# Three streams of one convolution pipeline, re-timed: taps paced by emitted work, attention begun a band earlier, rows loaded band by band

## The chip, the cores and the metric

The kernel runs on one core of a Trainium2 chip. The metric is the device time of one execution in microseconds (us). Three runs of the kernel before took 10178.35, 10182.17 and 10183.77 us, median 10182.17.

## The reference

Two layers over x of shape (32, 96, 56, 56), fp32. Layer 0 is an inverted bottleneck with squeeze-and-excite; layer 1 is a chain of Fourier attention, a deformable 3x3 convolution beside a plain one, and a batch norm over all 32 images.

```python
# layer 0
h = silu(bn(conv1x1(x, fake_quant(w1))))                 # 96 -> 576 channels
h = silu(bn(depthwise3x3(h, fake_quant(w2))))
s = sigmoid(se_w2 @ silu(se_w1 @ mean(h) + b1) + b2)
x = x + bn(conv1x1(h * s, fake_quant(w3)))               # 576 -> 96
# layer 1
mag = abs(rfft2(x)); ca = sigmoid(mlp(pooled convs of mag))     # per channel
sa = sigmoid(convs of (mean x, l2 x, resized mean of mag))      # per pixel
y = x * ca * sa
freq = resize(mean(abs(rfft2(y))))
aux = concat(y, coord, freq)
offset = conv3x3(aux); gate = sigmoid(conv(relu(conv3x3(aux))))
y_def = 9 taps of y sampled bilinearly at offset, times def_w
z = (1 - gate) * conv3x3(y) + gate * y_def
out = relu(batch_norm(z) + x)                            # statistics over all images
```

## The kernel before, in words

Every image goes through three stages, and three images are in work at once. The innermost is the **band loop** (`for n, (b, j) in enumerate(bands)`, L1134): image `b` is cut in 7 bands `j` of 8 rows. A band is done in two halves `h`, each in two groups of tiles. Beside it run two Python generators, `streams`: `second(b + 1)` is `attend` for the next image (squeeze, the 1x1 projection, two Fourier passes `dft_mag`, the small convolutions of the attention), and `first(b + 2)` is `hidden` for the image after that (expand on TensorE, depthwise taps on VectorE).

Engines run their queues in the order in which this Python code emits instructions (`manual_schedule`), so *when* a generator is advanced decides the order of work on every queue. The clock of that order is the **slot**: `pump()` (L1029) counts one slot up and advances the streams. A band has 17 slots (14 in the two halves, 3 at its end), an image 119. A `yield` in a generator is one slot. Slots are not equal in time: the band's own work on TensorE (the joint convolution L632 at the band's start, sampling L738, `deform` L757, transposes L724, base convolution L670) is put out in slots 0, 3, 7 and 10; slots 11 to 16 hold hardly any.

- `hidden` (L221): 9 units of 128 channels by 28 rows; a unit is 9 taps on VectorE (L284, L286), one a step, with the next unit's expand (L186, evacuated by ScalarE with silu at L190 into one of two buffers `hp`) put in between. `finish` (L238) applies silu and stores the unit as `h2d`. Before, the 81 taps of an image are spread evenly over its 119 slots (`due`, L1033).
- `attend` (L444): starts with `squeeze` (L304); then 4 projections of 14 rows (loads L333, matmuls L351 and L357, evacuation L362, residual on GpSimd L474, store to `x1d` L475); a Fourier pass (loads L380, matmuls L407 and L432); then a chain of small matmuls into one PSUM tile `acc` (L488 to L569). Each of them waits for ScalarE or VectorE to read what the one before it wrote: a **hop**. Then a second Fourier pass on the gated image and a last short chain (L593, L599) whose result `fqd` is the frequency row. Before, most hops are one slot apart.
- `refill` (L1056): loads rows of the next image's `x1d` into the one padded image `yp` (L611, on SyncE's queue), the spatial attention as `sab` (L613, on GpSimd's queue, two buffers), and later multiplies on VectorE (`attend_rows`, L619); then loads the frequency row (L623). Rows of image `b+1` overwrite rows of image `b` that are no longer read.
- `offsets` (L646): joint convolution of band `n + 2`, evacuation, the copy `at` on VectorE (L661), its store `od` on GpSimd's queue (L665), base convolution, the broadcast load `ht` on SyncE's queue (L681), two activations (L683, L684) and the store `hd` (L686). `weights_load` (L690) reads `hd` on SyncE's queue; `weights` (L704) multiplies on VectorE.

The **turn** is band 5 (`turn = NBD - 2`, L1023): from there `offsets` of band `n + 2` belongs to the next image, so its rows must be in `yp`. Before, at the turn `drain()` runs out what is left of both streams, `refill` and `flush` follow, and both streams are started anew for the next pair of images. The attention thus begins at band 5 (first work three slots on) and ends in band 3 of the next image, some 90 slots later; rows 0 to 37 are all loaded in slot 10 of band 4.

Of the kernel before, what the change touches and what calls it, by code (L numbers as in the profile page):

```python
# [20 lines left out]
RB = 8  # L21
# [9 lines left out]
PD = 2  # L31
# [45 lines left out]
WAIT = object()  # L77

# [142 lines left out]
def hidden(tc, p, x, xn, h2d, pooled, defer):  # L221


    nc = tc.nc
    w = p["w0"]

    def rows_of(x, half):
        xt = p["xt"].tile([C, (HH + 1) * W], FP, name="xt")
        r0 = half * (HH - 1)
        nc.sync.dma_start(xt, x[:, r0 : r0 + HH + 1].rearrange("c h w -> c (h w)"))  # L230
        return xt

    xts = p.pop("xts", None) or [rows_of(x, 0), rows_of(x, 1)]
    if not p.pop("expanded", False):
        for _ in expand(nc, p, xts, UNITS[0]):
            yield

    def finish(u, acc):  # L238
        ch = UNITS[u][0]
        flat = acc.rearrange("p h w -> p (h w)")  # L240
        nc.scalar.activation(flat, flat, AF.Silu, bias=w["sh2"][:, ch : ch + 1], scale=w["inv2"][:, ch : ch + 1],  # L241
                             accum_out=pooled[:, u : u + 1])
        nc.scalar.dma_start(h2d[u], flat)

    before = None
    for u, (ch, half) in enumerate(UNITS):
        h1 = p["h1"]
        if xn is not None and u in (5, 8):

            p.setdefault("xts", []).append(rows_of(xn, int(u == 8)))  # L250
        if u + 1 < len(UNITS):
            more = expand(nc, p, xts, UNITS[u + 1])
        elif xn is not None:
            more = expand(nc, p, p["xts"], UNITS[0])
            p["expanded"] = True
        else:
            more = iter(())
        acc = p["acch"].tile([128, HH, W], FP, name="acch")

        rows_of_tap = lambda dy: (int(half == 0 and dy == 0), HH - int(half == 1 and dy == 2))  # L260
        diag = p.get("diag")
        taps = [k for k in (4, 0, 1, 2, 3, 5, 6, 7, 8) if diag is None or k not in TPE]
        parts = []
        if diag is not None:
            for r0 in range(0, HH, ER):
                pt = bank(p)[:, :EW].rearrange("p (h w) -> p h w", h=ER)
                for i, k in enumerate(TPE):
                    dy, dx = divmod(k, 3)
                    lo, hi = rows_of_tap(dy)
                    lo, hi = max(r0, lo), min(r0 + ER, hi)  # L270
                    nc.tensor.matmul(pt[:, lo - r0 : hi - r0], diag[:, ch, i], h1[:, dy + lo : dy + hi, dx : dx + W],
                                     start=(i == 0), stop=(i == len(TPE) - 1))
                parts.append((slice(r0, r0 + ER), pt))
            yield
        for n, k in enumerate(taps):
            dy, dx = divmod(k, 3)
            lo, hi = rows_of_tap(dy)
            win = h1[:, dy + lo : dy + hi, dx : dx + W]
            wk = w["w2"][:, ch, k : k + 1]
            if n == 0:  # L280
                for rs, pt in parts:
                    nc.vector.scalar_tensor_tensor(acc[:, rs], win[:, rs], wk, pt, ALU.mult, ALU.add)
                if not parts:
                    nc.vector.tensor_scalar(acc, win, wk, None, ALU.mult)  # L284
            else:
                nc.vector.scalar_tensor_tensor(acc[:, lo:hi], win, wk, acc[:, lo:hi], ALU.mult, ALU.add)  # L286
            if n == 3 and before:
                finish(u - 1, before)
            if len(taps) - 8 < n < len(taps) - 1:
                next(more, None)  # L290
            yield
        for _ in more:
            pass
        before = acc
    defer(lambda: finish(len(UNITS) - 1, before))
# [8 lines left out]
def squeeze(nc, p, pooled):  # L304
# [6 lines left out]
    yield  # L311
    s1 = p["sp"].tile([RED, 1], FP, name="s1")
    nc.scalar.activation(s1, p1[:RED, 0:1], AF.Silu, bias=w["seb1"], scale=1.0 / HW)
    yield
    for ch in range(NCH):
        nc.tensor.matmul(p1[:, 8 + ch : 9 + ch], w["sew2"][:, ch], s1, start=True, stop=True)
    yield
# [3 lines left out]
    yield  # L321
# [45 lines left out]
def dft_mag(nc, p, src, gate=None):  # L367
# [28 lines left out]
    if gate is None:  # L396
        parts = p["sq"].tile([2 * WX, 2, NPB * V], FP, name="sq")[: 2 * H, :, : NG * W].rearrange("p k (g w) -> p k g w", g=NG)
        yield from wait(2)
# [21 lines left out]
    yield  # L420
# [3 lines left out]
    for q0 in range(0, NP // 2, NQB):  # L424
# [14 lines left out]
        yield  # L439
    p["magnitude"] = mag  # L440
    yield from at_conv(p, lambda: nc.scalar.activation(mag, mag, AF.Sqrt))


def attend(tc, p, b, x, h2d, pooled, x1, given=False):  # L444
# [5 lines left out]
    nc = tc.nc  # L450
    w = p["w"]
    if not given:
# [6 lines left out]
        for q in range(NQ):  # L459
# [4 lines left out]
            yield  # L464
            if q + 1 < NQ:
                first = project_loads(nc, p, h2d, q + 1, 0)
            next(outs)
            yield
            os = next(outs)
            if q + 1 < NQ:  # L470
                rows = [first, project_loads(nc, p, h2d, q + 1, 1)]
# [5 lines left out]
        yield from wait(2)  # L477
# [3 lines left out]
    yield from dft_mag(nc, p, x1)  # L481
    mag = p["magnitude"]

    pa = p["acc"].tile([128, 512], FP, name="acc")
# [3 lines left out]
    nc.tensor.matmul(pm, w["fold"], p["sums"].rearrange("p k w -> p (k w)"), start=True, stop=True)  # L488
# [3 lines left out]
    s3 = p["sp"].tile([H, 2, W], FP, name="s3")  # L492
    nc.scalar.activation(s3[:, 1], pm[:, W:], AF.Sqrt, bias=w["eps6"][:H], scale=1.0 / C)
    nc.scalar.mul(s3[:, 0], pm[:, :W], 1.0 / C)
# [11 lines left out]
    yield  # L506
# [6 lines left out]
    yield  # L513
# [8 lines left out]
    yield  # L522
# [4 lines left out]
    yield  # L527
# [4 lines left out]
    yield  # L532
# [6 lines left out]
    yield  # L539
# [6 lines left out]
    yield  # L546
# [9 lines left out]
    yield  # L556
# [13 lines left out]
    yield  # L570
# [3 lines left out]
    yield  # L574
# [19 lines left out]
    yield  # L594
    fy = p["sp"].tile([V, 2, W], FP, name="fy")
    nc.scalar.copy(fy.rearrange("p m w -> p (m w)"), pf)
    yield
    for m in range(2):
        nc.tensor.matmul(pz, w["rows2"][:, m], fy[:, m], start=(m == 0), stop=(m == 1))  # L599
    yield  # L600
# [45 lines left out]
def offsets(nc, p, yp, j, top, hid, ybs, hds):  # L646
# [11 lines left out]
    yield  # L658
# [19 lines left out]
    yield from wait(2)  # L678
# [277 lines left out]
def layers(tc, a, dp, x1d, zd, stats, far):  # L956
# [6 lines left out]
    nc = tc.nc  # L963
    B = x1d.shape[0]
    with ExitStack() as ctx:
        p = {"tc": tc, "dp": ctx.enter_context(tc.tile_pool(name="l1d", bufs=3, space=DRAM))}
# [25 lines left out]
        streams, later = [], []  # L992
# [31 lines left out]
        n_first = len(UNITS) * NTAP  # L1024

        def start(b, length):
            streams[:] = [[second(b + 1), 0, slot + 3], [first(b + 2), 0, slot, length]]

        def pump():  # L1029
            nonlocal slot  # L1030
            slot += 1
            for st in streams:
                due = slot - st[2] if len(st) == 3 else n_first * (slot - st[2]) / st[3]  # L1033
                while st[1] < due:
                    if next(st[0], None) is WAIT:
                        break
                    st[1] += 1
                    if len(st) == 3:
                        break
            later.sort(key=lambda e: e[0])  # L1040
            while later and later[0][0] <= slot:
                later.pop(0)[1]()

# [5 lines left out]
        def drain():  # L1049
            for st in streams:  # L1050
                for _ in st[0]:
# [81 lines left out]
        start(0, turn * (NTX + 3))  # L1133
        for n, (b, j) in enumerate(bands):  # L1134
            if j == 0:
                st = p["st"].tile([C, NBD, 6], FP, name="st")
            if j == turn:
                drain()
                refill(b + 1, j * RB - PD)
                flush()  # L1140
                start(b + 1, slots)
            more = find(n + 2) if n + 2 < len(bands) else iter(())
            next(more, None)
            release()
            for h in range(2):
# [3 lines left out]
                for i, group in enumerate(GROUPS):  # L1149
# [4 lines left out]
                    if i == 0:  # L1154
# [10 lines left out]
                        if b + 1 < B and j == turn - 1 and h == 1:  # L1165
                            refill(b + 1, turn * RB - PD)
# [365 lines left out]
```

## Time and profile before

| what | value |
|---|---|
| median of three runs | 10182.17 us |
| the profiled execution | 10207.2 us, span 10205.2 us |
| mean granted TensorE clock | 0.888 |
| first joint convolution at | 377.4 us |
| last instruction before the closing normalisation (chain starts) | about 9925 us |
| the closing normalisation (L1357 to L1365) | about 280 us, bound by its loads and stores |

So some 9,550 us are the band loop, 32 images of about 300 us. The costliest groups of VectorE, TensorE and GpSimd in it:

```profile
L286 DVE SCALAR_TENSOR_TENSOR acch<-hp,w,acch 128x1512 f32<-128x1512 f32 (+1 forms) x2250 | 4222.5, 1877 | 37.8
L632 PE MATMUL mm<-yp,c_jointW 104*128 104x448 f32 x4032 | 1729.9, 585 | 420.7 <-DMA yp<-fqd 296.2
L714 POOL COPY ybl<-yp 96x448 f32<-96x448 f32 x896 | 980.6, 1120 | 3598.6 <-PE mm L724 3598.6
```

A row gives line, engine, operation, tiles, shapes and count; then the busy time in us and the mean of one in ns; then the idle time of the engine just before these instructions, and who ended it. The first row is the depthwise taps: 2250 of 1.88 us, more than half of VectorE's work. An fp32 matmul of the program shows as two records, so 4032 records are 2016 matmuls.

### The profile page before, as it was taken

The numbers are of one execution on the slowest core, as the hardware profiler recorded it, in microseconds if no ns is written. First come the engines' busy times: TensorE is split into PE (matmuls) and PEld (weight loads), VectorE is DVE, ScalarE is ACT, GpSimd is POOL, SyncE is SP. The second block draws the span as 40 slices with busy tenths as digits, with TensorE's granted clock in tenths as the row PEclk, the third lists the DMA queues.
The fourth block names the chain that finished last, engine by engine and source line by source line (L and its number), as shares of the span: only waits on it lengthen the run. The fifth ranks groups of instructions, "written<-read, shape, count | busy, mean of one in ns | idle before, by whom it ended". The sixth has DMA issues, their size and how long they took to land. (4 is left out here: it accounts for less than half of the span.)

```text
span 10205.2 us, 129758 instructions
## 1 busy us (share of the span) xinstructions
PE 8493.2 (83%) x48374; PEld 5169.5 (51%) x48374; DVE 7226.4 (71%) x6948; ACT 5318.3 (52%) x10264; POOL 2490.8 (24%) x2642
## 2 busy tenths in 40 slices
PE   5888888888888888888888888888888888888870
PEld 3455555555555555555555555555555555555540
DVE  7677777777767777777777777777777777777323
ACT  2355555555555555555555555555555555555443
POOL 0122222222222222222222222223222222322110
PEclk9888989998888988898898898898889889988985
DMA  2455455555455555555555555555555555545449
GB/s 77 115 139 138 135 144 153 146 146 128 136 141 144 152 148 137 134 139 143 151 145 145 130 137 141 143 151 151 134 135 138 144 150 150 150 129 135 126 129 418
DMA packets 1069475, 1486.00 MB, mean 146 GB/s; under 512 B 590438, under 2 KB 840086, under 8 KB 1056550
## 3 DMA queue, kind: packets, MB, share of 16 engines
q1 hardware_dynamic: 858747, 985.20, 37.4%
q10 hardware_dynamic: 153803, 329.80, 8.9%
q0 software_dynamic: 56288, 162.60, 6.5%
q8 instruction: 388, 6.36, 0.3%
q14 instruction: 249, 2.04, 0.1%
HBM read 1064.29 MB, written 412.65 MB: 145 GB/s over the span
## 5 line engine op out<-in xcount | busy, mean ns | idle before, releaser
L286 DVE SCALAR_TENSOR_TENSOR acch<-hp,w,acch 128x1512 f32<-128x1512 f32 (+1 forms) x2250 | 4222.5, 1877 | 37.8
L632 PE MATMUL mm<-yp,c_jointW 104*128 104x448 f32 x4032 | 1729.9, 585 | 420.7 <-DMA yp<-fqd 296.2
L714 POOL COPY ybl<-yp 96x448 f32<-96x448 f32 x896 | 980.6, 1120 | 3598.6 <-PE mm L724 3598.6
L757 PE MATMUL pd<-v,c_def 128*96 128x224 f32 (+1 forms) x6272 | 1431.1, 385 | 64.4 <-DVE z L796 61.4
L632 PEld LDWEIGHTS mm<-yp,c_jointW 104*128 104x128 f32 x4032 | 812.3, 204 | 1261.0 <-issue 1158.4
L742 ACT COPY v<-mm 96x288 f32<-96x288 f32 (+1 forms) x2688 | 996.3, 442 | 805.7 <-PE mm L738 756.5
L757 PEld LDWEIGHTS pd<-v,c_def 128*96 128x96 f32 (+1 forms) x6272 | 1098.7, 179 | 427.3 <-issue 130.6
L190 ACT ACTIVATE hp<-mm,sh,inv 128x392 f32<-128x392 f32 (+2 forms) x1216 | 801.2, 673 | 892.1 <-PE mm L186 702.3
L186 PE MATMUL mm<-xt,w 96*128 96x392 f32 (+3 forms) x2688 | 1058.2, 546 | 51.6 <-DMA xt<-in_x 45.6
L738 PE MATMUL mm<-wc,yt 64*96 64x144 f32 x12544 | 1053.4, 302 | 31.5 <-ACT hp L190 16.3
L738 PEld LDWEIGHTS mm<-wc,yt 64*96 64x96 f32 x12544 | 837.8, 166 | 351.2 <-issue 175.8
L670 PE MATMUL mm<-yp,c_base0W 96*64 96x448 f32 x4032 | 974.5, 585 | 0.0
L726 ACT COPY yt<-mm 128x384 f32<-128x384 f32 (+1 forms) x896 | 348.8, 441 | 1060.7 <-PE mm L724 1060.1
L351 PE MATMUL mm<-hq,w3s 128*96 128x392 f32 x2048 | 740.5, 508 | 137.1 <-DMA hq<-h2d 105.9
L661 DVE COPY at<-mm 18x224 f32<-18x224 f32 x448 | 154.4, 380 | 972.8 <-ACT yb L657 970.2
L749 ACT COPY v<-v 32x448 f32<-32x448 f32 x1344 | 755.3, 562 | 40.7 <-ACT ht L684 16.2
L665 POOL DMA_DIRECT2D od<-at x224 | 185.1, 826 | 2286.3 <-DVE at L661 2095.4
L407 PE MATMUL mm<-c_FU,x 112*128 112x116 f32 x3072 | 443.6, 299 | 264.9 <-DMA x<-x1d 224.9
L241 ACT ACTIVATE acch<-acch,sh,inv 128x1568 f32<-128x1568 f32 x288 | 487.5, 1693 | 300.4 <-DVE acch L286 287.2
L704 DVE TENSOR_TENSOR wc<-wc,wr 128x1008 f32<-128x1008 f32 x448 | 591.8, 1321 | 25.0 <-PE mm L724 9.4
L670 PEld LDWEIGHTS mm<-yp,c_base0W 96*64 96x64 f32 x4032 | 339.1, 143 | 529.2 <-issue 454.8
L474 POOL TENSOR_TENSOR o<-o,xc 96x392 f32<-96x392 f32 x256 | 438.7, 1714 | 672.4 <-ACT o L362 622.0
(195 smaller groups left out, 9108.7 us busy)
## 6 DMA issues: line engine op xcount, KB each, us to landing
h2d<-acch ACTq DMA_DIRECT2D x288, 784.0 KB
wc<-hd SPq DMA_DIRECT2D x896, 252.0 KB
wr<-hd SPq DMA_DIRECT2D x896, 252.0 KB
hq<-h2d SPq DMA_DIRECT2D x128, 980.0 KB
hq<-h2d SPq DMA_DIRECT2D x128, 784.0 KB
x<-x1d SPq DMA_DIRECT2D x768, 98.0 KB
ht<-od SPq DMA_DIRECT2D x224, 252.0 KB
hd<-ht ACTq DMA_DIRECT2D x224, 252.0 KB
```

Source lines behind the costliest of these rows:

```text
L186: nc.tensor.matmul(pt[p0 : p0 + w1.shape[1], : rows * W], w1, xts[hf][:, r0 * W : (r0 + rows) * W], start=True, stop=True)
L190: nc.scalar.activation(h1[lo:hi, row0 : row0 + rows, 1 : 1 + W], pt[lo:hi, : rows * W].rearrange("p (h w) -> p h w", h=rows), AF.Silu, bia ...
L286: nc.vector.scalar_tensor_tensor(acc[:, lo:hi], win, wk, acc[:, lo:hi], ALU.mult, ALU.add)
L351: nc.tensor.matmul(pts[half][:C, :EW], w3s[:, ch], hq, start=(i == 0), stop=False)
L632: nc.tensor.matmul(view, weights[:, k], yp[:channels, r0 : r0 + RB, dx + PD - 1 : dx + PD - 1 + W], start=(k == 0), stop=(k == NTAP - 1))
L670: nc.tensor.matmul(pb[k % 2 * BC : (k % 2 + 1) * BC, :BW].rearrange("p (h w) -> p h w", h=RB), w["base"][:, k], yp[:C, r0 : r0 + RB, dx + ...
L704: nc.vector.tensor_tensor(wc, wc, wr, ALU.mult)
L714: nc.gpsimd.tensor_copy(yb[:, :, s], blocks)
L738: nc.tensor.matmul(pt[k][:C, (t - lo) * KP : (t - lo + 1) * KP], yt[ps, t], s[ps, t * KP : (t + 1) * KP], start=True, stop=True)
L742: nc.scalar.copy(v[:C, :, lo:hi, k].rearrange("c k t p -> c t k p"), pt[k][:C, : (hi - lo) * KP].rearrange("c (t k p) -> c t k p", t=hi - ...
L749: nc.scalar.copy(v[C:, 1 + 2 * i : 3 + 2 * i], v[i * QC : (i + 1) * QC, KA:])
L757: nc.tensor.matmul(out.rearrange("c q (t x) -> c t q x", x=TS), p["w"]["def"][ks, k], v[ks, k].rearrange("c t s (r x) -> c t (s r) x", r=T ...
```

## The change

1. **Pacing.** A `Clock` counts, at emission, an estimate of the TensorE and VectorE time of every instruction of the band loop (wrappers `Counted` and `Engines` around `nc.tensor` and `nc.vector`). The depthwise stream is no longer advanced by slots: at the end of each `pump` it is advanced until the emitted VectorE time since the start stands to the emitted TensorE time as 232.0 to 220.4.
2. **Start.** Both streams are drained and restarted at band 4 (`PHASE`), after that band's joint convolution is emitted, in place of band 5 before it.
3. **Hops.** 18 plain `yield`s in `squeeze`, `attend` and `dft_mag` become `yield from wait(2)`. The wait ahead of the first Fourier pass's matmuls is one slot shorter, the wait after the last projection one longer; projection loads are issued one slot earlier; in `offsets`, the `at` copy and with it the `od` store come one slot later, `ht` stays. The `fold` matmul and the l2 root move into the Fourier pass.
4. **Rows.** `refill` runs in bands 2, 3 and 4 (up to rows 22, 30, 38), in the first half, in place of once in band 4's second half (up to row 38).

The number of instructions of each kind is the same. Core of the diff:

```diff
+class Clock:
+    def count(self, engine, args):
+        free = lambda t: math.prod(t.shape[1:])
+        aps = [t for t in args if hasattr(t, "shape")]
+        if engine == "pe":
+            out, w = aps[0], aps[1]
+            share = 0.5 ** ((w.shape[0] <= 64) + (math.prod(w.shape[1:]) <= 64))
...
+            self.pe += max(max(free(out), 48) * 1.7e-3 * share, 0.158 if w.shape[0] == 64 and share == 0.5 else 0.0)
+        else:
+            self.dve += (max(map(free, aps)) + 180) / 960
...
@@ attend
             next(outs)
-            yield
             if q + 1 < NQ:
                 first = project_loads(nc, p, h2d, q + 1, 0)
+            yield
             next(outs)
+            if q + 1 < NQ:
+                rows = [first, project_loads(nc, p, h2d, q + 1, 1)]
             yield
...
-        yield from wait(2)
+        yield from wait(3)
...
@@ squeeze, dft_mag, attend: 18 times
-    yield
+    yield from wait(2)
...
@@ offsets
-    yield
+    yield from wait(2)
     at = p["off"].tile([NOFF, NTX, 2, TP], FP, name="at")
...
-    yield from wait(2)
+    yield
     ht = p["ht"].tile([SB * NTX, 4, KP], FP, name="ht")
...
@@ layers
-        def start(b, length):
-            streams[:] = [[second(b + 1), 0, slot + 3], [first(b + 2), 0, slot, length]]
+        PHASE, PE_IMAGE, DVE_IMAGE = NBD - 3, 220.4, 232.0
+        def start(b, share=1.0):
+            streams[:] = [second(b + 1), first(b + 2)]
+            paced[:] = clock.pe, clock.dve, share * PE_IMAGE
         def pump():
             slot += 1
-            for st in streams:
-                due = slot - st[2] if len(st) == 3 else n_first * (slot - st[2]) / st[3]
-                while st[1] < due:
...
+            next(streams[0], None)
             later.sort(key=lambda e: e[0])
             while later and later[0][0] <= slot:
                 later.pop(0)[1]()
+            while clock.dve - paced[1] < (clock.pe - paced[0]) / paced[2] * DVE_IMAGE:
+                if next(streams[1], paced) is paced:
+                    break
...
-        start(0, turn * (NTX + 3))
+        start(0, 0.83)
...
+            more = find(n + 2) if n + 2 < len(bands) else iter(())
             if j == turn:
-                drain()
                 refill(b + 1, j * RB - PD)
                 flush()
-                start(b + 1, slots)
-            more = find(n + 2) if n + 2 < len(bands) else iter(())
             next(more, None)
             release()
+            if j == PHASE:
+                drain()
+                start(b + 1)
...
-                        if b + 1 < B and j == turn - 1 and h == 1:
-                            refill(b + 1, turn * RB - PD)
+                        if b + 1 < B and 1 < j < turn and h == 0:
+                            refill(b + 1, (j + 1) * RB - PD)
```

## The prediction

> **What bounds the kernel now.** I read the page's first two parts, then the busy time by windows, then the waits of TensorE.
>
> ```profile
> PE 8493.2 (83%) x48374; PEld 5169.5 (51%) x48374; DVE 7226.4 (71%) x6948; ACT 5318.3 (52%) x10264; POOL 2490.8 (24%) x2642
> ...
> PEclk9888989998888988898898898898889889988985
> ```
>
> TensorE leads, no engine is full, and the granted clock stays near 0.9 throughout. The windows (columns: window, us, then busy us of PE, PEld, DVE, ACT, POOL, then granted clock, DMA share, GB/s):
>
> ```profile
> 1003.30:9426.90 8423.60, 7295.53 (x41936) 4443.64 (x41937) 6253.59 (x5769) 4558.52 (x8872) 2220.69 (x2296) 0.90 0.53 142
> 5205.00:5226.00 21.00, 8.74 (x39) 5.11 (x38) 16.50 (x13) 8.85 (x17) 4.84 (x6) 0.67 0.87 201
> 5083.00:5115.00 32.00, 23.93 (x147) 16.58 (x146) 20.95 (x27) 17.70 (x42) 3.07 (x5) 0.68 0.42 110
> 5267.00:5290.00 23.00, 23.00 (x106) 12.00 (x105) 5.92 (x6) 9.74 (x18) 10.79 (x14) 1.00 0.60 198
> ```
>
> The first is 28 images: 300.8 us each, TensorE busy 260.6, VectorE 223.3, so 40.2 us of TensorE idle. The second is one turn, the third one attention chain, the fourth a stretch without gaps. Where TensorE idles the clock is granted at 0.67, where it does not at 1.00. The clock records hold only the values 1.0 and 0.5: laid over the busy intervals, 61.8 us of each image run at half clock, 44.5 of them while TensorE is busy. That loses up to 44.5 / 2 = 22 us, so an image is about 238.5 us of matmul at full clock, 22 us of slow clock and 40 us of idle. Each us of idle drags 22/40 = 0.55 us of slow clock behind it. I check the 238.5: start-to-start times at full clock by row (joint convolution 2 x 0.389 us a matmul, deform 2 x 0.193, projection 2 x 0.342, ...) times the counts give 238.6. VectorE's 223 us are 15 us under it.
>
> The waits of TensorE between 400 and 9900 us, 31 images (total us, times, longest):
>
> ```profile
> PE mm L632 <- DMA yp<-fqd: 291.9, 26, 12.6
> PE mm L407 <- DMA x<-x1d: 222.4, 55, 6.9
> PE mm L351 <- DMA hq<-h2d: 102.1, 73, 4.9
> PE acc L538 <- ACT s L535: 67.7, 31, 2.5
> PE mm L632 <- ACT hp L190: 64.6, 29, 2.2
> PE pd L757 <- DVE z L796: 61.4, 38, 2.0
> PE mm L632 <- DVE acch L286: 59.9, 5, 12.7
> PE acc L316 <- ACT s L313: 55.4, 31, 3.2
> PE acc L518 <- ACT fe L508: 46.9, 31, 1.5
> PE acc L526 <- ACT t L524: 41.2, 30, 1.4
> PE acc L599 <- ACT fy L596: 36.7, 31, 1.4
> PE acc L563 <- ACT ca L562: 33.6, 31, 2.4
> ```
>
> Three things: the turn (rows 1 and 7), loads for the Fourier pass and the projection (2, 3), and the hops (`acc`). So the bound is TensorE's in-order queue, standing still at points where the emitted order brings a consumer too close behind its producer.
>
> **The change part by part.** Nothing is computed anew; what moves is the distance, in TensorE work, between producer and consumer. I took the new order from the built program and weighed each instruction with its row's mean of the trace before.
>
> *Turn and rows.* Before, rows 0 to 37 are asked for in slot 10 of band 4, and the joint convolution that reads them stands 7 slots on, with some 4 us of TensorE work between. After, the last rows it reads are loaded in band 2, 48 slots ahead, and the frequency row 14 slots ahead. Rows 1 and 7 go: (291.9 + 59.9) / 31 = 11.3 us an image. Each row chunk's issues (L611 median 0.53 us on SyncE, L613 about 0.51 us on GpSimd) are the same in number, only spread.
>
> *Drain.* Before, what is left of the taps is emitted in one lump at the turn. After, the streams end almost together: one or two taps are drained.
>
> *Pacing.* Emitted work by band, us of TensorE / VectorE, band 0 to 6. Before: 40/42, 31/38, 37/29, 27/33, 25/30, 36/30, 43/30. After: 27/24, 34/33, 30/31, 26/26, 33/29, 51/50, 37/39. The sum of the larger of each band is 259 before, 241 after. But before the waits on VectorE are small, so little of the 18 us is there to win: the waits for `hp`, `z` and ScalarE's evacuations, (64.6 + 61.4 + some 34) / 31 = 5.2 us an image. Bounds: 0 and 5.2; I take 2.5, half, as the balance cannot touch those that are pure distance.
>
> *Hops.* The `acc` waits add up to 350 us, 11.3 an image. Before, `sew2` has 2.1 us of matmuls between it and its producer and waits 1.8: the hop is about 3.9 us. After, 3.5 to 4.3 lie between: gone. L518 (4.6 us cover, 1.5 wait; after 8.6), L526 (half), L599 (no cover, 1.2; after 2.8 to 3.6), L563 (5.2, 1.1; after 10.5) go too: together 6.3 us. But a second slot is worth only what TensorE work is emitted in it: L538, L544 and L550 now fall in slots 13 to 17 of band 0, which hold none, and ScalarE's own work (L683, L684 at 0.78 us each, three packs of 0.56) stands in their hops. They keep their 3.9 us, and L569 now stands behind six taps (6 x 1.88 = 11.3 us on VectorE beside about 10 us on TensorE): I charge 3 us. Net 3.3; bounds 0 and 10.
>
> *Fourier loads.* All of the 7.2 us an image is at two places: the first group (2.7) and the sixth (5.4, where only two groups of 0.92 us stand between the buffer's release and its reuse). After, about 19 us of TensorE work stand between the last projection and the first group, against 15 + 2.7 = 17 needed: gone. The sixth stays: its buffer is released by VectorE's sums (L391), now behind five taps. Gain 2.2.
>
> *Projection loads.* A slot earlier and in the densest band (51 us): 102.1 + 25 over 31 is 4.1; I take 3.1.
>
> *Costs.* `od` is now behind the two block copies (2 x 1.1 us) on GpSimd's queue, and in band 2 behind a third `sab` load that waits for a buffer until `attend_rows`, three slots on. Then `ht`, L683 and `hd` come late. The trace shows `ht` landing 2 to 9 us after its issue and L683 never waiting (0.5 us in all), so I cost it at 0 to 5 us once an image and take 0, since ScalarE comes to L683 only at about 27 of band 2's 30 us. Image 0: its streams are drained in band 4 with some 42 of the attention's 112 slots left, serial, about 45 us once.
>
> *A rule against the row.* "TensorE: Matmul & The Clock Gate" of the Trainium skill (Why this matters for your kernels) says that only idle gaps over some 3 us throw the clock back to half. By it, of what I remove only the turn's waits count, and their half clock lies inside the idle itself: no clock comes back. The trace says otherwise: in the attention chain above no gap exceeds 1.9 us, yet the clock is 0.68, and 133 of 183 gaps of 1.5 to 2.5 us have half clock within 3.5 us. The measurement decides.
>
> *Sum.* Idle removed: 11.3 + 2.5 + 3.3 + 2.2 + 3.1 = 22.4 us an image. With 0.55 of slow clock: 34.7. Times 31: 1076 us. Against the profiled execution: 10207 - 1076 + 45 = 9176. The median of the runs stands 25 us under it: **9150 us**. By the rule the sum is 10182 - 31 x 22.4 + 45 = 9533.
>
> **Rivals.** *A, the waits nearly vanish.* Balanced bands and longer distances leave only matmul at full clock and about 11 us: 250 us an image, 10182 - 31 x 51 + 45 = 8650. For it: VectorE has 15 us to spare, and emitted VectorE never gains over 10 us on TensorE within a few slots. Against: the uncovered hops and the sixth Fourier group.
>
> *B, only the turn goes.* The hops and loads give back what they win, and the clock returns for the turn alone or as the rule says: 11 to 14 us an image: 10182 - 31 x 13 + 45 = 9820. For it: shorter slots give each DMA less time. Against: the distances in TensorE work, which grew.
>
> *C, slower.* The `at` copy (L661) frees the joint convolution's PSUM bank. It stands a slot later, behind 4 to 7 taps emitted together (7.5 to 13 us); six banks rotate, and the first half's sampling and transposes take eight, so TensorE stops there when VectorE is behind. Cover is about 11 us: the price is some 2 us a band as emitted. To lose the 34.7 it takes 5 us a band, 7 times. For it: VectorE waits 970 us for `yb` before L661 today, so that copy is on a chain. Against: taps need no fresh matmul and run ahead during the joint convolution.
>
> *D, the pacing does nothing.* The built order shows it does: the band table.
>
> **How the numbers follow.** Mine 0.52, A 0.20, B 0.20, C 0.07, D 0.01. The likeliest gives 9150. Bounds of the unknown costs (pacing 0 to 5.2, hops 0 to 10, `ht` 0 to 5; times 1.55 times 31) put my own case at 8750 to 9550; with half of A and of B outside, 8700 to 9750. This measurement tells 0.2% from no change (20 us). Faster 0.92, same 0.01, slower 0.07.
>
> **What would show it.** Right: the row of waits of the joint convolution for `yp` gone; granted clock 0.93 or more; about 265 us an image with VectorE near 85% busy; the waits that remain on `acc` from `s` and `c`, and on the sixth Fourier group. Wrong: waits of the sampling matmuls for `at`, idle time of ScalarE before L683 for `ht`, or a clock that stays at 0.89 with fewer gaps.

## The result, and the profile after

The changed kernel took 10486.6 us (median of 4 runs, 10478.73 to 10498.77) against 10182.97 (4 runs, 10178.35 to 10184.79): 1.030 times as long, interval 1.0282 to 1.0318. The prediction was 9150, and faster. The profiled execution has a span of 10476.8 us, 271.6 more than before.

From the first two parts of the page after:

```profile
PE 8579.5 (82%) x48374; PEld 5242.0 (50%) x48374; DVE 7446.0 (71%) x6948; ACT 5315.6 (51%) x10276; POOL 2650.2 (25%) x2642
...
PEclk9888989898998988989999898998889898989995
```

The span less TensorE's busy time is its idle time: 1712.0 us before, 1897.3 now. So 185 of the 271.6 us are new idle time; the other 86 are busy time of the same 48374 records. VectorE and GpSimd are busy for 220 and 159 us more, with the same instructions. The busy time by windows, for 28 images (window, us, then busy us of PE, PEld, DVE, ACT, POOL, clock, DMA share, GB/s):

```profile
1017.60:9675.20 8657.60, 7361.66 (x41947) 4504.03 (x41945) 6460.56 (x5768) 4561.47 (x8892) 2365.98 (x2296) 0.90 0.52 138
```

309.2 us an image against 300.8, TensorE busy 262.9 against 260.6, at the same 0.90 of the clock. The waits of TensorE between 400 and 10100 us (total us, times, longest; in this trace every TensorE and VectorE instruction of the band loop carries L109, the line of the wrapper, so one goes by the tiles):

```profile
PE mm L109 <- DMA hq<-h2d: 293.2, 74, 10.7
PE mm L109 <- POOL x L430: 163.2, 87, 5.1
PE acc L109 <- ACT ca L620: 158.1, 30, 5.5
PE mm L109 <- DMA x<-x1d: 136.0, 41, 6.1
PE pd L109 <- DVE z L109: 113.7, 28, 5.4
PE mm L109 <- ACT hp L235: 82.1, 58, 2.9
PE acc L109 <- ACT s L593: 64.2, 31, 2.2
PE acc L109 <- ACT t L582: 47.2, 17, 3.2
PE mm L109 <- ACT ht L742: 42.5, 15, 4.2
```

The turn's rows (`yp<-fqd`, `acch`, 351.8 us together) are gone, and the one for `x` fell. But `hq` went from 102.1 to 293.2, `z` from 61.4 to 113.7, `ca` from 33.6 to 158.1; and a row came that was not there before: the second Fourier pass waits for the gating on GpSimd (`x` at L430). The waits of the other queues in the same window name what changed behind them:

```profile
DVE acch L109 <- DMA h2d<-acch: 460.8, 44, 16.1
...
SPq L739 <- DMA od<-at: 2949.0, 161, 34.8
...
POOL sab L671 <- DVE yp L109: 305.9, 35, 14.6
```

The same two rows of SyncE and GpSimd in the trace before:

```profile
SPq L681 <- DMA od<-at: 1588.4, 130, 17.9
...
POOL sab L613 <- DVE yp L619: 372.6, 79, 9.5
```

VectorE now waits 461 us for the store of its own accumulator (`acch`), against 6.6 before (5.4 and 1.2, in two rows). SyncE stands longer at the `ht` load for `od`. GpSimd's wait at the `sab` load for a free buffer is not larger than before in all, but in fewer and longer pieces, and it stands at another place of the queue.

### The profile page after: what moved, and what is told of

It is laid out like the page before. It is cut to its first block, busy times and chain, and to the rows that moved or that the text cites. A ratio compares the mean times of both kernels' runs of the same rounds, so it can differ in the third digit from the quotient of the medians.

```text
span 10476.8 us, 129798 instructions
## 1 busy us (share of the span) xinstructions
PE 8579.5 (82%) x48374; PEld 5242.0 (50%) x48374; DVE 7446.0 (71%) x6948; ACT 5315.6 (51%) x10276; POOL 2650.2 (25%) x2642
## 5 line engine op out<-in xcount | busy, mean ns | idle before, releaser
L109 DVE SCALAR_TENSOR_TENSOR acch<-hp,w,acch 128x1512 f32<-128x1512 f32 (+1 forms) x2250 | 4449.4, 1978 | 112.9 <-ACT hp L235 52.8
L772 POOL COPY ybl<-yp 96x448 f32<-96x448 f32 x896 | 1064.8, 1215 | 5319.1 <-PE mm L109 5308.8
L109 PE MATMUL mm<-yp,c_jointW 104*128 104x448 f32 x4032 | 1687.1, 573 | 6.3 <-DMA yp<-fqd 6.3
L109 PE MATMUL pd<-v,c_def 128*96 128x224 f32 (+1 forms) x6272 | 1564.3, 410 | 124.3 <-DVE z L109 113.7
L109 PEld LDWEIGHTS pd<-v,c_def 128*96 128x96 f32 (+1 forms) x6272 | 1165.2, 192 | 452.4 <-DVE z L109 118.1
L109 PE MATMUL mm<-hq,w3s 128*96 128x392 f32 (+1 forms) x2560 | 915.5, 543 | 369.5 <-DMA hq<-h2d 294.8
L109 PEld LDWEIGHTS mm<-yp,c_jointW 104*128 104x128 f32 x4032 | 783.1, 199 | 816.6 <-issue 771.2
L109 PE MATMUL mm<-wc,yt 64*96 64x144 f32 x12544 | 1064.8, 298 | 144.8 <-ACT hp L235 59.1
L109 PEld LDWEIGHTS mm<-wc,yt 64*96 64x96 f32 x12544 | 832.1, 162 | 469.7 <-issue 207.1
L109 PE MATMUL mm<-xt,w 96*128 96x392 f32 (+3 forms) x2688 | 939.6, 517 | 48.4 <-DMA xt<-in_x 45.6
L109 PE MATMUL mm<-yp,c_base0W 96*64 96x448 f32 x4032 | 944.8, 572 | 13.5 <-ACT yt L784 13.5
L109 PEld LDWEIGHTS mm<-hq,w3s 128*96 128x96 f32 (+1 forms) x2560 | 385.8, 176 | 846.6 <-issue 704.0
L109 PE MATMUL mm<-c_FU,x 112*128 112x116 f32 x3072 | 518.0, 324 | 339.2 <-POOL x L430 167.4
L109 PEld LDWEIGHTS mm<-c_FU,x 112*128 112x128 f32 x3072 | 465.8, 230 | 469.4 <-POOL x L430 226.8
L109 DVE TENSOR_SCALAR acch<-hp,w 128x1568 f32<-128x1568 f32 x270 | 299.6, 1110 | 495.3 <-DMA h2d<-acch 460.8
L109 PEld LDWEIGHTS mm<-xt,w 96*128 96x128 f32 (+1 forms) x2688 | 410.9, 183 | 370.3 <-issue 215.8
L109 DVE TENSOR_TENSOR wc<-wc,wr 128x1008 f32<-128x1008 f32 x448 | 536.1, 1197 | 50.2 <-DMA wr<-hd 49.4
```

Of the source, the lines that this page charges most:

```text
L109: return do(*args, **kw)
L772: nc.gpsimd.tensor_copy(yb[:, :, s], blocks)
```

## The experiments

Eighteen kernels, each timed in three rounds beside the kernel before on the same chip; the figures are the ratio to that, with its 95% interval. A part that differs from one run to the next is read from the two ratios, since the kernel before itself took 10152 to 10183 us from one chip to another.

### Rows: one load too many in GpSimd's queue

**e1**, before with the change's `refill` alone:

```diff
-                        if b + 1 < B and j == turn - 1 and h == 1:
-                            refill(b + 1, turn * RB - PD)
+                        if b + 1 < B and 1 < j < turn and h == 0:
+                            refill(b + 1, (j + 1) * RB - PD)
```

> The kernel before with the row loading alone: chunks in bands 2, 3 and 4, first half. Theory 1 (the rows were late, and nothing else was wrong at the turn): the joint convolution's waits of 11.3 us an image go with 0.55 of slow clock each: 31 x 17.5 = 540 us faster, about 9640. Rival (the turn's wait hides another, the lump of taps that drain() puts out there): the wait for fqd only changes its name to taps or hp, under 150 us faster, about 10030 or more.

Measured: 10414.27 us, **1.0242** (1.021 to 1.0275). The waits of TensorE, then of GpSimd, in its trace:

```profile
PE mm L407 <- POOL x L385: 344.3, 31, 18.0
...
PE mm L632 <- DMA yp<-fqd: 4.5, 1, 4.5
```

```profile
POOL sab L613 <- DMA yp<-x1d: 302.9, 30, 11.8
```

The turn's wait went as it should, and 11 us an image came back at another place. In band 2 three `sab` loads are asked for and there are two buffers; the third stands in GpSimd's queue until `attend_rows` has freed one, and behind it, in the same queue, stands the sixth gating multiplication of the second Fourier pass, for which TensorE waits (all 344 us are at this sixth group). One image of the trace shows it: two `sab` loads are issued by 5220.9 us, `attend_rows` frees the first buffer at 5230.55, the third load follows at 5230.84 and the gating at 5231.37. The row of GpSimd names the load of `yp`, for which `attend_rows` waits as well (97.1 us in all).

**e5**, the same with one chunk of rows in each half, so that a third load is never asked for while two are held (in place of e1's two new lines):

```diff
+                        if b + 1 < B and 1 < j < turn:
+                            refill(b + 1, min((j + 1) * RB - PD, filled.get(("y", b + 1), 0) + RB))
```

> Before, with the rows of the next image asked for one chunk of a band at a time, one in each half of bands 2 to 4, so that GpSimd never has a third load of sab asked for while two are held. Theory 1 (the +240 us of the run that loaded the rows by bands came from GpSimd's in-order queue: a third sab load waits for a buffer and the second Fourier pass's gating stands behind it): the wait of the Fourier matmul for that gating, 344 us in that run, falls under 80 us, the turn's wait (292 us before) stays under 30 us, and the time falls under that of before, to 9640 to 9950 us. Rival (loading rows early costs by itself, by its DMA traffic or by VectorE's blend standing in front of the taps): the time stays at 10300 to 10450 us whatever the buffers do. In between (10000 to 10250): both, in proportion.

Measured: 10015.9 us, **0.9878** (0.9857 to 0.99). The waits do what theory 1 said, but the time lies above its 9640 to 9950, in the range that was named for both causes. TensorE's waits:

```profile
PE mm L632 <- DMA yp<-fqd: 5.0, 1, 5.0
...
PE mm L407 <- POOL x L385: 0.3, 1, 0.3
```

Both rows are all but gone at once. The same edit in the changed kernel, **e6**:

> The changed kernel, with the rows asked for one chunk at a time in each half of bands 2 to 4 instead of up to three at the start of a band. Theory 1 (GpSimd's queue blocked by the third sab load makes od late by up to 18 us in band 2 and with it ht, and holds the gating of the second Fourier pass): od leaves within 6 us of at in all bands, and the time falls by 150 to 350 us, to 10130 to 10330 us. Rival (what the change loses lies in the late start of the streams and in taps that stand in front of the producers): under 50 us of change, 10430 to 10550 us.

Measured: 10356.7 us, **1.0217** (1.0195 to 1.0239): 0.8% under the changed kernel, about 85 us: less than the 150 to 350 of theory 1, more than the 50 of the rival. The edit does what it should for the third load: ScalarE's wait for `ht` falls from 108.6 to 10.1 us, and in the joint convolution emitted in band 2 `od` leaves at 17.6 us from its start, not 27.9 (medians). But `od` does not leave within 6 us of `at` everywhere: for the joint convolution of band 3, `at` ends at 14.1 us and `od` leaves at 29.2 (before: 12.7 and 13.0), now behind the gating. And TensorE's wait for the gating stays, 164.7 us against 163.2: in the changed kernel it is not the third load that makes it. So most of the loss is elsewhere.

### Pacing, hops and start: each alone, then together

Three runs on the changed kernel as it is. **e2**, taps spread evenly over the slots instead of paced:

> The changed kernel with its taps spread evenly over the slots again (start, hops and rows as changed). Theory P (the pacing puts taps in dense runs, VectorE then waits for the store of its accumulator, 461 us, and z, hp and the projection loads come late): faster than the changed kernel by 300 us or more, at or under 10180. Theory S (the shift of the attention by a band and the doubled hops put the second Fourier pass and ca in slots without band work): within 100 us of the changed kernel, 10390 to 10590.

Measured: 10580.92 us, **1.0403** (1.0369 to 1.0438). **e4**, one slot a hop again:

> The changed kernel with one slot a hop again (18 waits; pacing, start at band 4 and rows as changed). Theory S: the second Fourier pass returns to other slots and the GpSimd waits of its matmuls (163 us) and the ca hop (158 us) fall: 300 us or more faster, 10190 or less. Theory P: within 150 us, 10330 to 10590. My prediction's own step (two slots a hop win 3.3 us an image) would make it 150 us slower.

Measured: 10484.99 us, **1.031** (1.0277 to 1.0343). Here pacing seems to help by 1% and hops to do nothing; neither theory's 300 us came. In e4 TensorE's wait for the gating did fall, from 163 to 8 us, but its waits on VectorE rose from 243 to 501 in all. **e3**, the store of a finished accumulator two taps earlier (`if n == 1 and before` in place of `n == 3`):

> The changed kernel with each unit's silu and store emitted after the next unit's second tap in place of its fourth. If VectorE's wait for the store of the accumulator (461 us in 44 waits) decides, it shrinks by 3.8 us a wait, 170 us or more, and the kernel is 100 to 250 us faster, about 10240 to 10390. If those waits lie in VectorE's slack, within 50 us of the changed kernel, or slower, as ScalarE now waits for the last tap.

Measured: 10350.22 us, **1.0175** (1.0144 to 1.0206). **e7**, e3's and e6's edits together:

> The changed kernel with both repairs: rows one chunk at a time, and the store of a finished accumulator issued after the second tap of the next instead of after the fourth. If the two losses are separate, the gains add: the run with single chunks less some 136 us, so 9990 to 10200 us. If both are one (VectorE's queue late), no more than 40 us under the better of the two alone.

Measured: 10196.32 us, **1.0056** (1.0035 to 1.0077): -1.25% and -0.83% alone, -2.4% together. Within the intervals they add.

Taking one part out of the whole does not tell what it costs, so the next runs put parts on e5. **e8** is the changed kernel with single chunks, streams started at the turn, one slot a hop; **e9** is e8 with even taps, so that only e5's rows and the small moves are left (`at` later, projection loads earlier, the first Fourier pass's distances, `fold` and the root moved; the attention also begins in the turn's first slot, not three later):

```diff
-            paced[:] = clock.pe, clock.dve, share * PE_IMAGE
+            paced[:] = slot, 0, share * slots
...
-            while clock.dve - paced[1] < (clock.pe - paced[0]) / paced[2] * DVE_IMAGE:
+            while paced[1] < len(UNITS) * NTAP * (slot - paced[0]) / paced[2]:
+                paced[1] += 1
```

> The changed kernel with single chunks, one slot a hop, and the streams drained and started at the turn (band 5, ahead of its joint convolution) as before, not 1.5 bands earlier. What is left of the change: pacing, rows by bands, projection loads a slot earlier, the at copy a slot later. If the early start is itself a loss (the attention's first hops and second Fourier pass fall into bands without taps or behind GpSimd work): 100 to 400 us under the run with single chunks, down to 9700 to 10050 us. If the early start is neutral or good: the same as that run within 60 us, or above it, since the first projection waits for nothing that the early start did not give.

> The run with single chunks and streams started at the turn (1.017 of before), with the taps spread evenly over the slots in place of the pacing. It then differs from before with single chunks (0.988) in the small moves alone: the at copy, the projection loads, the levels and roots of the spatial maps. Theory P (pacing by emitted time costs where the attention starts at the turn, since it emits taps ahead of the attention's own VectorE steps): 10020 to 10120 us, 0.987 to 0.997 of before. Rival M (the small moves cost, the at copy first): it stays at 1.010 or more, 10250 us and above.

Measured: e8 10318.16 us, **1.017** (1.0151 to 1.019); e9 9939.21 us, **0.9794** (0.9774 to 0.9814). The pacing alone loses 380 us; the small moves win 0.8%. The waits of TensorE in e8, then those in e9:

```profile
PE acc L109 <- DVE qs L109: 143.5, 30, 5.8
...
PE mm L109 <- DVE yb L109: 100.0, 37, 3.9
...
PE mm L109 <- DVE sq L109: 68.5, 58, 2.6
```

```profile
PE mm L396 <- DMA hq<-h2d: 182.7, 31, 8.0
PE mm L452 <- DMA x<-x1d: 169.8, 32, 8.3
PE acc L559 <- DVE m_fe L551: 139.7, 31, 4.8
```

With pacing, TensorE waits for VectorE's steps, those of the attention (`qs`, `sq`) and of the band (`yb`): all its waits on VectorE are 552 us in e8, 286 in e9. That they come late because taps stand ahead of them is read from these rows and the emitted order; no run moved those steps alone. Of the 14.2 us an image between the two traces, 8.4 are idle time and 5.9 busy time: with pacing, TensorE is busy at half clock for 51.2 us an image, without it for 40.0. The accumulator's store is a small part of it: **e18**, e8 with e3's edit.

> The pacing with single chunks, small moves, streams started at the turn, hops of one slot (1.017 of before), with the store of a finished accumulator issued after the second tap of the next. If the pacing loses by VectorE's wait for that store (283 us in that run, none with even taps): 0.985 to 0.995. If it loses by taps that stand ahead of the attention's own VectorE steps and beside GpSimd's work: 1.005 to 1.017.

Measured: 10272.53 us, **1.0112** (1.0089 to 1.0134), 0.6% of the 3.8%. VectorE's wait for the store stayed at 263 us there, so the edit did not take the wait away, and what the wait is worth at the turn is open.

**e10**, e5 with the 18 hops doubled (`yield` to `yield from wait(2)`), and **e11**, e5 with the early start alone:

> Before with single chunks (0.988 of before), and the 18 hops of the attention doubled to two slots, as the change has them. The prediction's size of the hops: 3.3 us an image of idle time less, so 100 to 160 us faster, 0.972 to 0.978 of before. Theory that a hop only moves its wait (the waits on acc fall, but steps behind them now meet bands with less work): within 40 us of the run with single chunks, 0.984 to 0.992. Rival: slower, above 0.995, since the later maps hold up the second Fourier pass and the turn.

> Before with single chunks (0.988 of before), and only the early start added: streams drained and begun in band 4, behind its joint convolution, taps spread evenly as before. If the early start is the part that loses (the projection meets loads that have had no time, the second Fourier pass falls at the end of band 1): 1.010 to 1.035 of before, 10250 to 10500 us, with the wait for hq at or above 200 us and the one for the gating above 100. If it is neutral: 0.985 to 0.993. If it gains (the maps end earlier, so rows are never late): below 0.985.

Measured: e10 11157.35 us, **1.0992** (1.0967 to 1.1016); e11 9988.53 us, **0.9835** (0.9815 to 0.9855). By the emitted order, the doubled stream of e10, started at the turn, gives the spatial attention only in band 3, so no rows can be loaded in band 2, and its last chain is run out in one slot at the next turn, as this wait of TensorE shows:

```profile
PE acc L593 <- DVE m_fy L589: 413.6, 28, 15.5
```

So the hops need the early start; what they cost beside it is the next square. The early start alone costs nothing (e11; but 0.7% beside the small moves, e13 below). **e12**, the late `at` copy alone on e5, is the test of rival C:

> Before with single chunks (0.988 of before), and only the at copy of the offsets moved one slot later, ht where it was. The prediction's rival C: the copy frees the joint convolution's PSUM bank later and the offsets reach the sampling later; some 2 us a band, or 217 bands x 1 to 2 us = 200 to 400 us slower, 1.005 to 1.03. If the cover holds: within 30 us, 0.985 to 0.991.

Measured: 10045.54 us, **0.9893** (0.9872 to 0.9913). The cover holds with even taps. C spoke of taps in bunches, which e12 has not; there the traces answer: TensorE waits 7.0 us for `at` in the changed kernel and 83.4 in e6, at most 2.7 us an image. Rival C is not the cause.

**e13** (e9 with the early start), **e14** (and doubled hops), **e15** (early start and pacing); e6 is the fourth corner:

> Single chunks and the small moves (0.979 of before), with the early start added; taps even, hops of one slot. If the early start is as neutral as without the small moves (-0.4%): 0.973 to 0.980. If the small moves and the early start collide (the projection's loads, a slot earlier, meet the last taps' store): above 0.985, with the wait for hq above 200 us.

> The changed kernel with single chunks and even taps: early start and doubled hops, no pacing. Theory P (pacing is the part that loses everywhere): 0.975 to 0.99. Theory H (the doubled hops lose, because they push the second Fourier pass into slots that carry no band work and VectorE's steps there stand behind taps): 1.015 to 1.035, since the run of even taps with the rows by bands in one go stood at 1.040 and single chunks are worth about 1%.

> The changed kernel with single chunks and hops of one slot: early start and pacing. Theory P (pacing loses by itself): 1.015 to 1.03, as the one-slot run without single chunks (1.031) less 1%. Theory H (the hops lose, pacing is neutral with the early start): 0.975 to 0.99.

Measured: e13 10043.77 us, **0.9862** (0.9838 to 0.9887); e14 10438.18 us, **1.0261** (1.0236 to 1.0286); e15 10498.14 us, **1.0324** (1.0295 to 1.0354). Beside the early start, doubled hops lose 4.0%, pacing loses 4.6%, and both together (e6, 1.0217) 3.6%. That is why taking out one of them left the time where it was.

Per image, from the traces (mean of the 31 periods from one image's first joint convolution to the next's, us; one execution each, on several chips, so differences under some 1 us say nothing):

| run | rows | added | period | PE idle | PE busy |
|---|---|---|---|---|---|
| before | | | 300.6 | 40.5 | 260.1 |
| e5 | single | | 294.0 | 32.8 | 261.2 |
| e11 | single | early start | 294.0 | 33.2 | 260.8 |
| e9 | single | small moves | 291.7 | 32.0 | 259.7 |
| e8 | single | small moves, pacing | 305.9 | 40.4 | 265.6 |
| e13 | single | small moves, early start | 296.0 | 35.1 | 260.9 |
| e14 | single | the same, hops | 307.7 | 40.9 | 266.8 |
| e15 | single | the same as e13, pacing | 309.8 | 46.5 | 263.3 |
| e6 | single | the same as e13, hops, pacing | 305.1 | 42.8 | 262.3 |
| after | at once | all | 309.2 | 46.7 | 262.5 |

By way of e5, e9, e13 and e6, the change's +8.6 us an image are -6.6 (rows in time), -2.3 (small moves), +4.3 (early start with them), +9.1 (hops and pacing) and +4.1 (the third load; 2.7 by the ratios). Another order would share them out otherwise: on e5 alone the early start is worth 0.

### Where the doubled hops lose

In e14, TensorE waits for the gating again, though no third `sab` load is in the way:

```profile
PE mm L452 <- POOL x L430: 177.2, 100, 5.5
```

In the emitted order the gating of an image begins at slot 263 (slot 8 of band 1) in place of 253 (slot 15 of band 0, e13). From 253 the joint convolution of the next band stands between it and the Fourier groups, from 263 little does; in one image of the traces the first group follows the start of its gating by 5.7 us in e13 and by 2.0 in e14. How long a gating takes shows in its row by tile (count, then ns shortest/median/longest), here first of before, then of after:

```profile
L385 POOL TENSOR_TENSOR x<-x,sa x192: 1126/1821/2682, 329.0 to 9621.9; 112x448 f32<-112x448 f32 x192
```

```profile
L430 POOL TENSOR_TENSOR x<-x,sa x192: 1119/2604/3126, 343.2 to 9897.7; 112x448 f32<-112x448 f32 x192
```

One instruction, 1.1 to 3.1 us. Laid over VectorE's records: with VectorE idle it takes 1.13 us (14 of 192 after, 38 before); where taps fill more than half of it, 2.28 on the mean after and 2.00 before. Six groups at 2.6 are 15.6 us of GpSimd for one pass. The Trainium skill ("SBUF — State Buffer", Who interferes with whom) says that a VectorE instruction with two SBUF inputs, as a tap is (`hp` and `acch`), and a GpSimd instruction that reads SBUF contend for shared ports, which are an exclusive lock: one of the two waits. A tap is some 1.85 us, so by that page a gating that loses once should take at most about 1.13 + 1.85 = 2.98 us, an estimate; the longest after is 3.13. The trace agrees on the size, and shows the other side too: the longest tap takes 5.37 us (2.72 before), and gatings under such taps take their 1.1 us. It is not always one loss: in e4 a gating takes up to 5.4 us. But slowness alone is not the cause: beside taps the gating takes 2.66 in e9 and 2.67 in e13, where TensorE hardly waits for it, and 2.03 in e14. What the doubled hops took away is the TensorE work in front of it; that was read from the order and not tried by a run of its own. And the gating is at most about half of what they cost: of 11.7 us an image between e13 and e14, 5.8 are idle time and 5.9 busy time, with half clock while TensorE is busy up from 44.7 to 55.5 us.

**e16** lengthens three distances of e9 where its waits stand:

> The run with single chunks and small moves (0.979 of before), with three distances lengthened where its trace shows a wait at one place once an image: the second half of the first projection's rows loaded five slots sooner (hq, 183 us), three slots more before the first Fourier group (x, 170 us), one slot more behind the sum m_fe (140 us). If these waits are pure distance: 250 to 500 us faster, 0.93 to 0.955. If the work is only moved and other waits take their place: within 80 us, 0.971 to 0.987.

Measured: 10072.08 us, **0.9903** (0.9878 to 0.9927), slower than e9 and outside both expectations. Its longest waits of TensorE:

```profile
PE mm L396 <- DMA hq<-h2d: 185.8, 31, 8.5
PE mm L452 <- DMA x<-x1d: 171.5, 32, 7.6
PE mm L452 <- POOL x L430: 149.2, 31, 5.6
```

`m_fe` left the list. The totals of `hq` and `x` did not move, for two different reasons that show when the waits are counted by place. That of `hq` stands, in e9 and e16 alike, at the second half of the *second* projection, whose load the edit does not touch. That of `x` did go where the distance was lengthened, at the first Fourier group (166.4 us in e9, none in e16), and came back at the sixth (none in e9, 171.2 in e16). And with the gating one slot on, GpSimd waited 403 us for its loads of `x` (e9: 89) and TensorE 149 us for the gating, though this ran quicker than in e9 (median 1.14 us against 1.87), not beside more of VectorE's work as the next expectation has it. **e17** takes the wait for `m_fe` alone and closes up a later hop, so that the gating keeps its slot:

> The run with single chunks and small moves (0.979 of before) with one edit: one slot more behind the sum m_fe, whose consumer waits 140 us in all, and the hops behind it closed up by one slot, so that the gating and all behind it keep their slots (in the run with three longer distances they moved by one slot, the gating came beside more of VectorE's work, and the wait for it rose from 0 to 149 us). If a wait can be taken out where nothing else moves: m_fe under 10 us, the gating under 20, and 60 to 150 us faster, 0.965 to 0.974. If the slots' work is what counts: no faster than 0.976.

Measured: 9918.13 us, **0.9755** (0.9732 to 0.9779): it beats both kernels, but its interval overlaps e9's. Its longest waits of TensorE:

```profile
PE mm L396 <- DMA hq<-h2d: 192.9, 31, 8.2
PE mm L452 <- DMA x<-x1d: 187.5, 34, 9.5
PE acc L584 <- DVE qs L570: 112.7, 30, 4.5
```

The 140 us of `m_fe` are gone and 113 of `qs`, the next hop, have come. The wait for the gating stayed under 20 us. Of 140 us of wait, at most 20 to 40 were time, by the medians and by the ratios, and that is not clear of noise: TensorE's waits together are 996 us in e9 and 1013 in e17.

## Why the prediction was wrong

Step by step, as it put them:

- *Turn and rows*: the wait went as predicted (351.8 us before, 5.0 in e5, no row left in the changed kernel). Its price did not: in e5, 11.3 us an image of removed wait are 7.7 us less idle time and 6.6 us of period, not 11.3 x 1.55 = 17.5. Of e5's other waits some grew; and the factor failed, see below.
- *Costs, `od` and the third `sab` load, "take 0"*: it named the load that waits and followed `od`, `ht` and ScalarE, and there 0 to 5 us was a fair bound (e6: 0.8%, 2.7 us an image; one of its signs of being wrong, ScalarE waiting for `ht`, came with 108.6 us). It did not follow GpSimd's own queue to the gating behind it. On the kernel before that is the step that fails: in e1 it costs 344 us of TensorE waits and turns -1.2% into +2.4%.
- *Pacing, "bounds: 0 and 5.2"* and *hops, "bounds 0 and 10"*: the steps that failed for the sign. The lower bound was an assumption that longer distances and balanced bands cannot lose. Measured beside the early start: 4.6% and 4.0% lost, 3.6% for both.
- *In the pacing*, what the runs show is the store of the accumulator (e3 and e7: 1.2% to 1.6% of the changed kernel, e18: 0.6% at the turn) and more waits on VectorE's own steps. The balance of *emitted* time per band (259 to 241) said nothing of the order inside a slot. How the rest of the loss divides stays open, and so does whether another ratio than 232.0 to 220.4 would lose less; no run tried one.
- *In the hops*, the waits that they were to take away grew: the `acc` rows together are 389 us in e13 and 430 in e14, 372 before and 471 in the changed kernel. `sew2` and L599 went as predicted (55.4 to 7.2 and 36.7 to 7.3 us), L538, L544 and L550 stayed, also as predicted; but L563 (`ca`), which was to go, waits 158.1 us after 33.6. The doubled hops also move the second Fourier pass to slots where no TensorE work covers the gating (177 us in e14). The other half of their loss is slower busy time, of which the prediction had nothing.
- *Projection loads, 3.1*: the other way, 102.1 to 293.2 us, 240.8 of them at the second half of the first projection. Already e9 has 182.7, in 31 waits, one an image, at the second half of the second.
- *Fourier loads, 2.2*: the sum was right (222.4 to 136.0 us is 2.8 us an image), by luck. The first group's wait, which was to go, rose from 78.9 to 118.4 us; the sixth's, which was to stay, fell from 143.5 to 8.9.
- *Drain, 45*: image 0 takes 38.8 us longer, about right. The first joint convolution also begins 20.7 us later; so it does in every run with doubled hops (396 to 404 us) and in none without (374 to 381), a term that the prediction did not have.
- *The factor 1.55*: an average taken for a slope. From before to e5, idle time fell by 7.7 us an image and TensorE's busy time rose by 1.1; after the change idle time rose by 6.2, and half clock fell from 61.8 to 60.6 us. In e5 half clock fell to 54.4 us, but the part of it in which TensorE is busy, which alone costs matmul time, went from 44.5 to 45.5: what fell lay inside the removed gaps. The rule that the prediction set against the row said just that of the turn, and is nearer to what was measured, though the short gaps with half clock behind them are in the trace all the same.
- *The range*: the bounds as they are listed add up to 8700 to 9670 us, not 8750 to 9550. The result lies outside either.

Rival C had the right sign and the wrong place: the `at` copy is covered in e12 and hardly waited for in the changed kernel. D was wrong; the pacing does much.

## What to carry to other kernels

A step that is moved needs a bound on the losing side too: name what stands behind it on each in-order queue at its new place, compute that shares a queue with a transfer above all. Never ask for more loads on a compute queue than there are buffers for them at that moment. And measure parts on the kernel before as well as by leaving them out of the whole: two parts that lost 4.0% and 4.6% alone lost 3.6% together, and each looked harmless when only it was taken out. Before you lengthen a distance, count its wait by place: in e16 one row's total stood still while its wait moved from the first group to the sixth.

## What the runs showed of the hardware

- The same GpSimd multiply takes 1.13 us with VectorE idle, 2.60 at the median in the changed kernel, and up to 5.4 us in e4. The taps pay too: 1877 ns on the mean before, 1978 after, as these rows of the page after show (busy us, mean ns, then idle before):

```profile
L109 DVE SCALAR_TENSOR_TENSOR acch<-hp,w,acch 128x1512 f32<-128x1512 f32 (+1 forms) x2250 | 4449.4, 1978 | 112.9 <-ACT hp L235 52.8
...
L772 POOL COPY ybl<-yp 96x448 f32<-96x448 f32 x896 | 1064.8, 1215 | 5319.1 <-PE mm L109 5308.8
```

- The block copies of GpSimd rose likewise, from 1120 to 1215 ns. No edit changed either instruction.
- The amount of half clock is no function of idle time alone: 66.2 us an image with 40.9 idle (e14), 61.8 with 40.5 (before), 60.6 with 46.7 (after).
